# Products of constants ahead of the chains of layer 0's FFN and layer 2's routing

## The chip, the core and the metric

The kernel runs on one core of one Trainium2 chip. The metric is device time in microseconds (us) of that core for one execution; a kernel's time is the median of its runs.

## What is computed

Four layers work in turn on x of 4 x 512 x 128 numbers in float32. Each is FFN, attention, FFN, each with a residual. The change touches the two passes of layer 0's FFN and the two of layer 2's:

```python
# layer 0's FFN: three selections, one row per sequence of the batch (4 rows)
input_acts_seq = gelu(einsum('bsd,nd->bsn', x, input_patterns)).mean(axis=1)      # 4 x 1024
input_repr = the 128 largest of each row, zero elsewhere
process_acts = gelu(einsum('bn,pn->bp', input_repr, process_input_weights))       # 4 x 512
process_weights = softmax(the 64 largest of each row)
aggregated_value = einsum('bk,bkd->bd', process_weights, selected_process_values) # 4 x 64
output_acts_seq = gelu(einsum('bd,od->bo', aggregated_value, output_input_weights))  # 4 x 1024
out_per_seq = the 128 largest of each row, weighted sum of their output_patterns  # 4 x 128, to all 512 rows
# layer 2's FFN: each of the 2048 rows goes to the one expert of 8 with the largest probability
top1 = argmax(softmax(x @ router_w + router_b))
out = (a * sigmoid(g)) @ w2[top1] + b2[top1],  a, g = split(x @ w1[top1] + b1[top1])
```

## The kernel before, in words

The rows of x stand as 16 tiles of 128 rows by 128 features. All is float32; a float32 product of TensorE leaves two matmul records in the trace. PSUM is divided into banks of 128 x 512 by tag ("s": 4, "t": 2, "m": 2 in layer 0; "a": 2, "g": 2, "t": 2, "m": 2 in layer 2's FFN).

**Layer 0's FFN** (`l0_ffn`). For each sequence eight 512-column products (pa, through `mm_in_order`) are followed by a gelu on ScalarE that sums over the rows. Then the work is one chain for all four sequences:

- `largest` finds the 128 largest of each row of 1024. VectorE takes the eight largest of a list of 256 and strikes them out, 16 times (lines 386 to 390), merges the sorted lists (394 to 401), turns the limit by a small transpose on TensorE (pt_l, line 403), and settles ties by two 32-column products (place, 421 and 422).
- The selected values go through eight 512-column products on four groups of array columns (pp, line 440), two copies and one product that adds the four groups (pp again, 445).
- After a gelu on ScalarE, VectorE finds the 64 largest of 512 in eight rounds (451 to 456); softmax, a transpose (pt_w, 466), the products pg (472) and po (478), a gelu.
- `largest` once more, with the transpose pt_c (line 369) beside its first round; then po (484), a copy, and pb (489), which spreads the four results; VectorE adds them to x.

**Layer 2's FFN** (`l2_slots`). After the router's logits VectorE finds each row's expert as a one-hot (oh, line 1262) and a running count over tiles (cum). Three products give each row's position (pos, 1276 to 1278). From pos VectorE works out the expert of each of 23 slots of 128 rows (ei) and the place of each row in its slot (place, in_slot). Sixteen 23-column products then turn this around into the list of rows that come to each slot (pi, 1317; come, 1319). SyncE loads the weights of a slot's expert (line 1326, five buffers; needs ei), GpSimd fetches the slot's rows by indirect DMA (1330, four buffers; needs come), TensorE transposes them (pt_x) and multiplies.

**Order.** A scheduler orders the instructions of each engine, save those handed to `keep_in_program_order`, which keep the order in which the program states them. `mm_in_order` and `transpose_in_order` are so pinned, `mm` and `transpose` are not. `idle_product(tag, n)` is a product of constants (onesm and the first n columns of cst) into a bank that nobody reads; before the change only layer 1's attention calls it.

Of the kernel before, what the change touches and what calls it, by code (L numbers as in the profile page):

```python
# [28 lines left out]
P = 128  # L29
B, S, D, H, HD = 4, 512, 128, 16, 8  # L30
NT = B * S // P
# [72 lines left out]
def tile_macaron(ctx, tc, x_in, const_in, vec_in, w0_in, ws_in, ws3_in, w2f_in, w3_in, out):  # L104
# [17 lines left out]
    def bank(tag, name):  # L122
        n = 2 if tag == "d" else 1
        return psum["pool"].tile([P, n * 512], F32, tag=tag, name=name, bufs=psum["bufs"][tag])
# [31 lines left out]
    def const(name):  # L156
        return CONST(cst, name)
# [6 lines left out]
    def mm(dst, lhsT, rhs, start=True, stop=True):  # L164
        nc.tensor.matmul(dst, lhsT=lhsT, rhs=rhs, start=start, stop=stop)

    def transpose(dst, src):
        return nc.tensor.transpose(dst, src, ident[: src.shape[0], : src.shape[0]])  # L168

    def mm_in_order(dst, lhsT, rhs, start=True, stop=True):  # L170
        tc.keep_in_program_order(nc.tensor.matmul(dst, lhsT=lhsT, rhs=rhs, start=start, stop=stop))  # L171

    def transpose_in_order(dst, src):
        tc.keep_in_program_order(transpose(dst, src))

    def idle_product(tag, n):

        mm_in_order(bank(tag, "idle")[:, :n], onesm, cst[:, :n])

    def bcast(ap, n):  # L180

        return ap[:, :, None].to_broadcast([ap.shape[0], ap.shape[1], n])
# [161 lines left out]
    def l0_ffn(tag, chained):  # L344
        with pool(tag) as sb:
# [18 lines left out]
            def by_neuron(row, name):  # L364

                r = sb.tile([P, 8, B], F32, tag="by_n", name=name, bufs=2)
                pt = bank("t", "pt_c")
                for c in range(2):
                    transpose(pt[:, ts(c, P)], row[:, ts(c, P)])
                nc.vector.tensor_copy(  # L370
                    r.rearrange("p (q c) b -> p c q b", q=4),
                    pt[:, :256].rearrange("p (c q b) -> p c q b", c=2, q=4)[:, :, :, :B],
                )
                return r
# [7 lines left out]
            def largest(row, vals, r):  # L382

                w = sb.tile([P, 256], F32, tag="w256", name="w256")
                order = sb.tile([P, P], F32, tag="order", name="order")
                for i in range(P // 8):
                    m8, src = order[:, ts(i, 8)], w if i else row
                    nc.vector.max(m8, src)
                    if i < P // 8 - 1:
                        nc.vector.match_replace(w, m8, src, GONE)  # L390
                two = [sb.tile([64, P], F32, tag=f"two{i}", name="two") for i in range(2)]
                larger(two[0], order, 64, 64)
                for i in range(7):
                    halves = [t.rearrange("p (n i k) -> p n i k", i=2, k=64 >> i) for t in (two[i % 2], two[1 - i % 2])]
                    for to, op in enumerate((ALU.max, ALU.min)):
                        nc.vector.tensor_tensor(halves[1][:, :, to, :], halves[0][:, :, 0, :], halves[0][:, :, 1, :], op)
                turned = sb.tile([B, P], F32, tag="turned", name="turned")
                larger(turned, two[1], B, 32)
                limit = sb.tile([B, 1], F32, tag="limit", name="limit")
                nc.vector.tensor_reduce(limit, turned, AX.X, ALU.min)  # L400
                nc.vector.tensor_copy(turned, limit.to_broadcast([B, P]))
                pt = bank("t", "pt_l")
                transpose(pt[:, :B], turned)
                lim = sb.tile([P, B], F32, tag="lim", name="lim")
                nc.vector.tensor_copy(lim, pt[:, :B])
                above, equal = (sb.tile([P, 8, B], F32, tag=n, name=n) for n in ("above", "equal"))
                nc.vector.tensor_tensor(equal, vals, rows(lim, 8), ALU.is_equal)
                nc.vector.tensor_tensor(above, vals, rows(lim, 8), ALU.is_gt)
                many = sb.tile([P, B], F32, tag="many", name="many")
                nc.vector.tensor_reduce(many, above.rearrange("p c b -> p b c"), AX.X, ALU.add)  # L410

                sums = [sb.tile([P, 8, B], F32, tag=f"sums{i}", name="sums") for i in range(2)]
                nc.vector.tensor_copy(sums[0][:, 0, :], many)
                nc.vector.tensor_copy(sums[0][:, 1:, :], equal[:, :7, :])
                for i in range(3):
                    n, src, dst = 1 << i, sums[i % 2], sums[1 - i % 2]
                    nc.vector.tensor_copy(dst[:, :n, :], src[:, :n, :])
                    nc.vector.tensor_add(dst[:, n:, :], src[:, n:, :], src[:, : 8 - n, :])
                place = bank("m", "place")
                flat = lambda v: v.rearrange("p c b -> p (c b)")  # L420
                mm(place[:, : 8 * B], const("m1"), flat(equal), True, False)
                mm(place[:, : 8 * B], ones, flat(sums[1]), False, True)
                nc.vector.scalar_tensor_tensor(
                    equal, place[:, : 8 * B].rearrange("p (c b) -> p c b", b=B), float(P), equal, ALU.is_le, ALU.mult
                )
                nc.vector.tensor_add(above, above, equal)
                nc.vector.tensor_mul(r[:, :, :B], above, vals)

            pt = bank("t", "pt_a")
            for c in range(2):  # L430
                transpose(pt[:, ts(c, P)], acc[:, c, :, :].rearrange("p q b -> p (q b)"))
            nc.vector.tensor_scalar_mul(ra, pt[:, :256], 1.0 / S)
            vals = sb.tile([P, 8, B], F32, tag="by_n", name="vals", bufs=2)
            nc.vector.tensor_scalar_mul(vals.rearrange("p (q c) b -> p c q b", q=4), acc[:, :, :, :B], 1.0 / S)
# [2 lines left out]
            p4 = bank("m", "pp4")  # L437
            piw = W0(w0, "piw").rearrange("p (c n) -> p c n", n=512)
            for c in range(8):
                mm(p4[ts(c % 4, 32), :], kept[0][:, c, :], piw[:, c, :], c < 4, c >= 4)  # L440
            pq = sb.tile([P, 512], F32, name="pq4")
            nc.vector.tensor_copy(pq[:, 0:256], p4[:, 0:256])
            nc.vector.tensor_copy(pq[:, 256:512], p4[:, 256:512])
            pp = bank("m", "pp")
            mm(pp[:B, :], selb.rearrange("p (b n) -> p b n", n=P)[:, :, 0], pq)
            pa = sb.tile([B, 512], F32, name="pact")
            nc.scalar.activation(pa, pp[:B, :], AF.Gelu)

# [2 lines left out]
            for i in range(KP // 8):  # L451
                m8 = sb.tile([B, 8], F32, tag=f"m8{min(i, 1)}", name="m8", bufs=2)
                nc.vector.max(m8, w if i else pa)
                nc.vector.match_replace(w, m8, w if i else pa, GONE)
                if i == 0:
                    nc.vector.tensor_scalar_mul(nm, m8[:, 0:1], -1.0)
            ea = sb.tile([B, 512], F32, name="ea")
            nc.scalar.activation(ea, pa, AF.Exp, bias=nm)
            sm = sb.tile([B, 1], F32, name="sm")
# [3 lines left out]
            nc.vector.tensor_scalar_mul(pw, pw, sm)  # L463
            pt = bank("t", "pt_w")
            for c in range(4):
                transpose(pt[:, ts(c, B)], pw[:, ts(c, P)])
            pwT = sb.tile([P, 4, B], F32, name="pwT")
            nc.vector.tensor_copy(pwT, pt[:, : 4 * B].rearrange("p (n b) -> p n b", b=B))
            pg = bank("m", "pg")
            pv = W0(w0, "pv").rearrange("p (c n) -> p c n", n=64)  # L470
            for c in range(4):
                mm(pg[:64, :B], pv[:, c, :], pwT[:, c, :], c == 0, c == 3)
            nc.vector.tensor_copy(agg[:, :B], pg[:64, :B])

            oiw = W0(w0, "oiw")
            po = bank("m", "po0")
            for q in range(4):
                mm(po[ts(q, 32), :256], agg, oiw[:64, ts(q, 256)])
            nc.scalar.activation(oa, po[:, :256], AF.Gelu)
            largest(oa, by_neuron(oa, "out"), kept[1])  # L480
            po = bank("m", "po1")
            op = W0(w0, "op").rearrange("p (c n) -> p c n", n=D)
            for c in range(8):
                mm(po[ts(c % 4, 32), :D], kept[1][:, c, :], op[:, c, :], c < 4, c >= 4)
            o4 = sb.tile([P, D], F32, name="o4")
            nc.vector.tensor_copy(o4, po[:, :D])
            pb = bank("m", "pb")
            for b in range(B):
                mm(pb[:, ts(b, D)], selb[:, ts(b, P)], o4)

            def update(b):
                xb = x[:, ts(b, TB), :]
# [765 lines left out]
    def l2_slots(sb, ticks, gap):  # L1258
# [3 lines left out]
        oh = first_max(sb, g, "oh")  # L1262


        cum = [sb.tile([P, NT, 8], F32, name=f"cum{i}") for i in range(2)]
        src = oh
        for i in range(4):
# [5 lines left out]
        nc.vector.tensor_sub(before, src, oh)  # L1273
        pos = bank("m", "pos")
        flat = lambda v: v.rearrange("p t e -> p (t e)")
        mm(pos[:, 128:136], ones, src[:, NT - 1, :])
        mm(pos[:, 0:128], ones, flat(before), True, False)
        mm(pos[:, 0:128], const("m1"), flat(oh), False, True)

        ni = sb.tile([P, 8], I32, name="ni")  # L1280
        nf, base, end = (sb.tile([P, 8], F32, name=n) for n in ("nf", "base", "end"))
        nc.vector.tensor_scalar_add(ni, pos[:, 128:136], float(P - 1))
# [28 lines left out]
        in_slot = sb.tile([P, NT, SLOTS], F32, name="in_slot")  # L1311
        nc.vector.tensor_tensor(in_slot, rows(const("iota")[:, :SLOTS], NT), bcast(slot, SLOTS), ALU.is_equal)
        nc.vector.tensor_mul(in_slot, in_slot, bcast(const("row1"), SLOTS))
        pi = bank("m", "pi")
        for t in range(NT):
            nc.vector.tensor_scalar(in_place[:, t, :], const("iota"), place[:, t : t + 1], None, ALU.is_equal)
            mm(pi[:, :SLOTS], in_place[:, t, :], in_slot[:, t, :], t == 0, t == NT - 1)
        come = sb.tile([P, SLOTS], I32, name="come")
        nc.vector.tensor_scalar(come, pi[:, :SLOTS], -1.0, 0.0, ALU.add, ALU.max)

# [760 lines left out]
```

## Time and profile before

| | us |
|---|---|
| median of 3 runs | 2732.9 |
| lowest and highest run | 2726.75, 2735.28 |
| the profiled execution, its time | 2729.0 |
| its span, first to last instruction | 2726.9 |
| TensorE busy | 2191.1 |
| VectorE busy | 1808.4 |
| ScalarE busy | 1267.1 |
| mean granted TensorE clock | 0.88 |

The page of the profile cuts the span into 40 slices of some 68 us. Its digits are busy tenths; PEclk is the clock that TensorE was granted, in tenths of full speed. In the timeline each row has a start and a length in us, the engine (PE: TensorE's products, PEld: its weight loads, DVE: VectorE, ACT: ScalarE, POOL: GpSimd, SPq: SyncE's queue), the line, the operation with what it writes and reads, how many were merged, and in brackets the idle time before and who ended it. A matmul of the program is x2 there. The table of stretches gives for each stretch, after its length, the busy time of PE, PEld, DVE, ACT and POOL, then the granted clock, the mean share of the DMA engines and GB/s. The first pass of layer 0's FFN ends its products pa at about 50 us and pb at 126, the second at 308 and 384; layer 2's passes have their pos at 1218 and 1454.

### The profile page before, as it was taken

The page shows a single profiled execution, that of the slowest core. Times are in us where ns is not written, and L with a number is a line of the kernel's source. Part 1 is how long each engine was busy: PE and PEld are TensorE (multiplying, and loading weights), DVE is VectorE, ACT ScalarE, POOL GpSimd, SP SyncE. Part 2 cuts the span into 40 slices and gives each one's busy share as a digit, 9 for nine tenths or more (in the row PEclk, how much of TensorE's full clock was granted, in tenths as well). Part 3 has the DMA queues.
Part 4 walks back from the last instruction along what each step waited for, and adds up shares of the span by engine and source line. Part 5 has one row for each costly group of instructions (what it writes and reads, how often), then busy time and mean ns, then how long its engine had stood idle before and what let it go on. Part 6 is the DMA issues. An engine that isn't in the chain of part 4 may idle for free. (4 is left out here: it accounts for less than half of the span.)

```text
span 2726.9 us, 49905 instructions
## 1 busy us (share of the span) xinstructions
PE 2191.1 (80%) x18572; PEld 1226.1 (45%) x18572; DVE 1808.4 (66%) x5013; ACT 1267.1 (46%) x3067; POOL 905.4 (33%) x1678
## 2 busy tenths in 40 slices
PE   4277539988779999948666868898899999789888
PEld 2145214443334444438456745555433333455555
DVE  4746487777566777563664487777567775877774
ACT  3054314444333544314332356776525554667764
POOL 1012012233122222213321377766300000877761
PEclk8578769998789999868886889999879999899998
DMA  3053010000000000008104611000000000100000
GB/s 143 0 158 93 0 63 1 1 1 1 1 1 1 1 2 5 5 21 300 37 10 160 200 27 24 21 21 20 1 0 1 1 1 7 28 20 21 22 21 12
DMA packets 33930, 99.31 MB, mean 36 GB/s; under 512 B 6200, under 2 KB 12344, under 8 KB 33176
## 3 DMA queue, kind: packets, MB, share of 16 engines
q1 hardware_dynamic: 30760, 88.03, 10.0%
q0 software_dynamic: 2496, 5.12, 0.8%
q8 instruction: 146, 2.39, 0.4%
q10 hardware_dynamic: 432, 2.98, 0.3%
q14 instruction: 96, 0.79, 0.1%
HBM read 66.88 MB, written 14.55 MB: 30 GB/s over the span
## 5 line engine op out<-in xcount | busy, mean ns | idle before, releaser
L832 ACT ACTIVATE PT<-pk_at 128x512 f32<-128x512 f32 (+3 forms) x768 | 335.2, 488 | 405.4 <-PE pq_at L171 259.3
L171 PE MATMUL pk_at<-qx,km 32*128 32x512 f32 (+3 forms) x1536 | 398.8, 554 | 4.6 <-ACT PT L832 2.7
L804 DVE CUSTOM_DVE_ANT_0 s<-pq_at,cst 128x384 f32<-128x384 f32 (+3 forms) x512 | 249.9, 488 | 96.0 <-PE pq_at L171 42.5
L171 PE MATMUL pq_at<-km,qT 32*128 32x128 f32 (+3 forms) x1024 | 274.0, 500 | 16.0 <-DVE nm L804 12.0
L1607 ACT ACTIVATE s<-s,nm,rn 128x128 f32<-128x128 f32 x512 | 245.5, 482 | 0.9 <-DVE nm L1719 0.7
L835 POOL TENSOR_SCALAR_AFFINE_SELECT PT<-PT 128x256 f32<-128x256 f32 x256 | 104.5, 410 | 388.7 <-ACT PT L832 387.7
L171 PEld LDWEIGHTS pk_at<-qx,km 32*128 32x128 f32 x1536 | 146.7, 190 | 153.3 <-issue 92.9
L171 PE MATMUL po_at<-PT,vh 128*32 128x128 f32 (+3 forms) x2432 | 205.6, 394 | 8.5 <-POOL PT L835 8.4
L806 DVE TENSOR_REDUCE nm<-pq_at 128x1 f32<-128x512 f32 x256 | 165.6, 685 | 57.6 <-PE pq_at L171 57.2
L1668 POOL TENSOR_TENSOR t<-t,t 128x1024 f32<-128x1024 f32 x64 | 151.8, 2372 | 123.4 <-DVE t L1664 123.1
L171 PE MATMUL pq_at<-km,t 32*128 32x512 f32 x512 | 175.0, 670 | 1.6 <-DVE nm L806 1.2
L168 PE MATMUL pt_y<-ident,y 128*128 128x128 f32 x224 | 52.3, 362 | 132.2 <-DVE y L225 104.9
L171 PE MATMUL p_qk<-w,hT 128*128 128x512 f32 x256 | 141.9, 682 | 8.8 <-DVE t L1664 6.0
L254 ACT COPY yT<-pt_y 128x512 f32<-128x512 f32 x56 | 32.8, 585 | 239.1 <-PE pt_y L168 238.6
L168 PE MATMUL pt<-ident,s 128*128 128x128 f32 x640 | 93.0, 293 | 62.0 <-POOL s L1731 38.9
L1731 POOL TENSOR_TENSOR s<-s,sm 128x1024 f32<-128x1024 f32 x64 | 121.6, 1901 | 49.1 <-DVE sm L1730 41.0
L171 PEld LDWEIGHTS po_at<-PT,vh 128*32 128x32 f32 x2432 | 53.8, 109 | 173.3 <-issue 119.8
L171 PEld LDWEIGHTS pq_at<-km,qT 32*128 32x128 f32 x1024 | 110.2, 189 | 46.6 <-DVE nm L804 26.8
L1607 ACT ACTIVATE sq<-p_qk 128x1024 f32<-128x1024 f32 x64 | 65.6, 1026 | 118.4 <-PE p_qk L171 65.8
L168 PEld LDWEIGHTS pt<-ident,s 128*128 128x128 f32 x640 | 78.2, 150 | 93.7 <-POOL s L1731 48.1
L1661 DVE TENSOR_TENSOR t<-p_qk,w 128x1024 f32<-128x1024 f32 x64 | 78.2, 1223 | 55.7 <-ACT sq L1607 55.6
L1349 DVE SCALAR_TENSOR_TENSOR hT<-pa,w,sg 128x128 f32<-128x128 f32 x184 | 51.9, 345 | 85.4 <-ACT sg L1348 63.6
(435 smaller groups left out, 5167.6 us busy)
## 6 DMA issues: line engine op xcount, KB each, us to landing
w<-in_w2f_dram SPq DMA_DIRECT2D x46, 836.0 KB, 6.2
vb<-v SPq DMA_DIRECT2D x112, 128.0 KB, 2.2
skew<-qe SPq DMA_DIRECT2D x16, 512.0 KB, 3.0
rel<-skew SPq DMA_DIRECT2D x64, 128.0 KB, 3.5
w<-in_w_dram SPq DMA_DIRECT2D x1, 4147.0 KB, 12.5
w<-in_w_dram SPq DMA_DIRECT2D x1, 3200.0 KB
od<-o SPq DMA_DIRECT2D x46, 64.0 KB, 5.1
yd<-y SPq DMA_DIRECT2D x8, 256.0 KB, 2.3
```

What stands on the lines that cost most here:

```text
L168: return nc.tensor.transpose(dst, src, ident[: src.shape[0], : src.shape[0]])
L171: tc.keep_in_program_order(nc.tensor.matmul(dst, lhsT=lhsT, rhs=rhs, start=start, stop=stop))
L254: by_order(nc.scalar.copy(yT[:, b, :], pt))
L804: nc.vector.tensor_tensor_reduce(s[:, :nk], pq[:, :nk], causal[:, S - nk :], 1.0, -BIG, ALU.add, ALU.max, to)
L806: nc.vector.tensor_reduce(to, pq, AX.X, ALU.max)
L832: by_order(nc.scalar.activation(PT[:, i, q0:], pk[:, q0:], AF.Exp, scale=SC8))
L835: nc.gpsimd.affine_select(d, d, pattern=[[0, 2], [1, P]], base=0, channel_multiplier=-1, compare_op=ALU.is_ge, fill=0.0)
L1349: nc.vector.scalar_tensor_tensor(hT[s][:, c, :], pa[:, ts(c, P)], b1[:, c : c + 1], sg, ALU.add, ALU.mult)
L1607: tc.keep_in_program_order(nc.scalar.activation(*args, **kw))
L1661: nc.vector.tensor_mul(by_head(t1), by_head(p3), over(tab[:, 0]))
L1668: nc.gpsimd.tensor_add(t1, t1, t2)
L1731: nc.gpsimd.tensor_mul(s, s, bcast(sm, P))
```

## The change

A helper `warm(gate, n)` issues a small product that reads `gate`, and n 512-column `idle_product`s after it; all of them are pinned. As TensorE works in order, none starts before `gate` is written. It is called after the maxima of the last six of the 16 rounds of `largest`, with four more products behind the last; after the last four of the eight rounds of the selection of 64, with one more behind; and in the routing after oh (three), after pos (three, not gated) and after place (one). In layer 0 the banks are of tag "s", in layer 2 of tag "a". All products and transposes of these chains are now pinned too.

```diff
+    def warm(gate, n, tag="s"):
+
+        mm_in_order(bank(tag, "idle")[:, : gate.shape[1]], onesm[: gate.shape[0], :], gate)
+        for _ in range(n):
+            idle_product(tag, S)
+
...
                     nc.vector.max(m8, src)
                     if i < P // 8 - 1:
                         nc.vector.match_replace(w, m8, src, GONE)
+                    if i >= P // 8 - 6:
+                        warm(m8, 1)
+                for _ in range(4):
+                    idle_product("s", S)
...
-                transpose(pt[:, :B], turned)
+                transpose_in_order(pt[:, :B], turned)
...
-                mm(p4[ts(c % 4, 32), :], kept[0][:, c, :], piw[:, c, :], c < 4, c >= 4)
+                mm_in_order(p4[ts(c % 4, 32), :], kept[0][:, c, :], piw[:, c, :], c < 4, c >= 4)
...
                 if i == 0:
                     nc.vector.tensor_scalar_mul(nm, m8[:, 0:1], -1.0)
+                if i >= KP // 8 - 4:
+                    warm(m8, 1)
+            idle_product("s", S)
...
         oh = first_max(sb, g, "oh")
...
+        warm(oh[:, 0, :], 3, "a")
...
-        mm(pos[:, 128:136], ones, src[:, NT - 1, :])
-        mm(pos[:, 0:128], ones, flat(before), True, False)
-        mm(pos[:, 0:128], const("m1"), flat(oh), False, True)
-
+        mm_in_order(pos[:, 128:136], ones, src[:, NT - 1, :])
+        mm_in_order(pos[:, 0:128], ones, flat(before), True, False)
+        mm_in_order(pos[:, 0:128], const("m1"), flat(oh), False, True)
+
+        for _ in range(3):
+            idle_product("a", S)
...
         nc.vector.tensor_mul(in_slot, in_slot, bcast(const("row1"), SLOTS))
+        warm(place, 1, "a")
         pi = bank("m", "pi")
         for t in range(NT):
             nc.vector.tensor_scalar(in_place[:, t, :], const("iota"), place[:, t : t + 1], None, ALU.is_equal)
-            mm(pi[:, :SLOTS], in_place[:, t, :], in_slot[:, t, :], t == 0, t == NT - 1)
+            mm_in_order(pi[:, :SLOTS], in_place[:, t, :], in_slot[:, t, :], t == 0, t == NT - 1)
```

The other transposes and products of the two chains (pt_a, pt_c, pt_w, place, pg, po, pb and the second pp) are pinned in the same way.

More of the change, by code (lines that the diff above doesn't have):

```diff
@@ L368, in by_neuron @@
                 for c in range(2):
-                    transpose(pt[:, ts(c, P)], row[:, ts(c, P)])
+                    transpose_in_order(pt[:, ts(c, P)], row[:, ts(c, P)])
                 nc.vector.tensor_copy(
@@ L420, in largest @@
                 flat = lambda v: v.rearrange("p c b -> p (c b)")
-                mm(place[:, : 8 * B], const("m1"), flat(equal), True, False)
-                mm(place[:, : 8 * B], ones, flat(sums[1]), False, True)
+                mm_in_order(place[:, : 8 * B], const("m1"), flat(equal), True, False)
+                mm_in_order(place[:, : 8 * B], ones, flat(sums[1]), False, True)
                 nc.vector.scalar_tensor_tensor(
@@ L430, in l0_ffn @@
             for c in range(2):
-                transpose(pt[:, ts(c, P)], acc[:, c, :, :].rearrange("p q b -> p (q b)"))
+                transpose_in_order(pt[:, ts(c, P)], acc[:, c, :, :].rearrange("p q b -> p (q b)"))
             nc.vector.tensor_scalar_mul(ra, pt[:, :256], 1.0 / S)
@@ L444, in l0_ffn @@
             pp = bank("m", "pp")
-            mm(pp[:B, :], selb.rearrange("p (b n) -> p b n", n=P)[:, :, 0], pq)
+            mm_in_order(pp[:B, :], selb.rearrange("p (b n) -> p b n", n=P)[:, :, 0], pq)
             pa = sb.tile([B, 512], F32, name="pact")
@@ L465, in l0_ffn @@
             for c in range(4):
-                transpose(pt[:, ts(c, B)], pw[:, ts(c, P)])
+                transpose_in_order(pt[:, ts(c, B)], pw[:, ts(c, P)])
             pwT = sb.tile([P, 4, B], F32, name="pwT")
@@ L471, in l0_ffn @@
             for c in range(4):
-                mm(pg[:64, :B], pv[:, c, :], pwT[:, c, :], c == 0, c == 3)
+                mm_in_order(pg[:64, :B], pv[:, c, :], pwT[:, c, :], c == 0, c == 3)
             nc.vector.tensor_copy(agg[:, :B], pg[:64, :B])
@@ L477, in l0_ffn @@
             for q in range(4):
-                mm(po[ts(q, 32), :256], agg, oiw[:64, ts(q, 256)])
+                mm_in_order(po[ts(q, 32), :256], agg, oiw[:64, ts(q, 256)])
             nc.scalar.activation(oa, po[:, :256], AF.Gelu)
@@ L483, in l0_ffn @@
             for c in range(8):
-                mm(po[ts(c % 4, 32), :D], kept[1][:, c, :], op[:, c, :], c < 4, c >= 4)
+                mm_in_order(po[ts(c % 4, 32), :D], kept[1][:, c, :], op[:, c, :], c < 4, c >= 4)
             o4 = sb.tile([P, D], F32, name="o4")
@@ L488, in l0_ffn @@
             for b in range(B):
-                mm(pb[:, ts(b, D)], selb[:, ts(b, P)], o4)
+                mm_in_order(pb[:, ts(b, D)], selb[:, ts(b, P)], o4)
             def update(b):
```

## The prediction

> **What bounds the kernel now.** I read the page first, for the engines and the clock row; then the timeline of the four places that the diff touches; then the table of stretches, cut to the steps in which the clock moves.
>
> ```profile
> span 2726.9 us, 49905 instructions
> PE 2191.1 (80%) x18572; PEld 1226.1 (45%) x18572; DVE 1808.4 (66%) x5013; ACT 1267.1 (46%) x3067; POOL 905.4 (33%) x1678
> PEclk8578769998789999868886889999879999899998
> ```
>
> TensorE carries the span, but not here: in slice 2 it is busy 2 tenths at clock 5. The two layer 0 FFNs (50 to 126 us, and 308 to 384) and the two routings (1216 to 1237, and 1452 to 1473) are single chains, VectorE handing to TensorE and back, so each microsecond of either is a microsecond of the end. The timeline (start, length, engine, operation, in brackets the idle time before and who ended it):
>
> ```profile
> 61.10 0.43 DVE L388 MAX8 order<-w 128x8 f32<-128x256 f32 x1
> ...
> 70.62 0.21 DVE L401 COPY turned<-limit 4x128 f32<-4x128 f32 x1
> ...
> 70.89 0.26 PE L168 MATMUL pt_l<-ident,turned 4*128 4x4 f32 x1 [20.13 <-DVE turned L401]
> ...
> 74.55 3.64 PE L165 MATMUL pp<-w,kept 128*32 128x512 f32 x16 [0.85 <-PE place L165]
> ...
> 79.15 1.87 PE L165 MATMUL pp<-pq,cst 128*4 128x512 f32 x2 [0.96 <-DVE pq L443]
> ...
> 337.38 1.02 PE L165 MATMUL pp<-pq,cst 128*4 128x512 f32 x2 [0.96 <-DVE pq L443]
> ```
>
> pt_l comes after 20 us without a product. The last two rows are one product in the first FFN and in the second: 1.87 us at half clock, 1.02 us at full. That halving is all there is to win. When does the clock move? (Stretch, then busy time of PE, PEld, DVE, ACT, POOL, then PEclk.)
>
> ```profile
> 73.73:77.14 3.41, 2.59 (x16) 0.68 (x16) 0.57 (x3) 0.00 (x0) 0.00 (x0) 0.50 0.02 5
> 138.59:142.00 3.41, 3.41 (x5) 0.96 (x3) 2.33 (x7) 0.67 (x1) 0.00 (x0) 0.50 0.38 154
> 142.00:145.41 3.41, 0.83 (x5) 0.42 (x4) 1.86 (x7) 2.52 (x5) 0.00 (x0) 1.00 0.25 77
> 333.14:336.56 3.42, 3.28 (x16) 0.45 (x8) 0.08 (x1) 0.00 (x0) 0.00 (x0) 0.50 0.00 0
> 336.56:339.97 3.41, 1.02 (x2) 0.12 (x2) 1.55 (x5) 0.59 (x1) 0.00 (x0) 1.00 0.00 0
> ```
>
> All its changes lie on one grid of 3.41 us. At each grid point the stretch just ended decides: 3.28 us of products at half clock bring full clock, 2.59 don't; 1.02 or 0.83 us at full clock lose it. I weighted every product by its columns and its share of the 128x128 array and put all 793 stretches of the trace against the next one's clock: a limit at three quarters of what a stretch can hold at half clock is right in 786. So a stretch needs 2.56 us of full-array products at half clock to rise, 1.28 us at full clock to hold; weight loads and thin products count little.
>
> **The change, part by part.** All of it is on TensorE's queue. The instruction order of the two builds is the same on the other four engines; on TensorE only the new products come in, and pinning the chain's products moves none. VectorE gets two waits more per FFN (a maximum waits until the small product has read its buffer of two rounds ago); at the rounds below that product is over 1 us earlier, so nothing. What queues behind the new products is the chain's next product, as TensorE works in order.
>
> Prices: a 512-column product is two records; they start 1.71 us apart per product at half clock (138.59 to 140.30), 0.855 at full (ten records of pa in 4.45 us). A small one: 0.42 us at half (pos, 1217.78 to 1218.20), so 0.21; if half of its loads hide behind the product before, perhaps 0.12 (an estimate). I take 0.21, the row's.
>
> The ramp: the products start at any point of the grid step. With 2.56 us or more of it left (1 case in 4) the clock rises at its end, else one step later: after 2.6 to 6.0 us, mean 4.3.
>
> *First selection of 128.* From the first gated maximum (61.53) to pt_l's operand (70.83) are 9.3 us. Put in there: 6 x (0.21 + 0.855) + 4 x 0.855 = 9.8 us at full clock, and half of the ramp on top. TensorE is free 0.5 + ramp/2 too late: 1.8 to 3.5 us, mean 2.6 (2.1 with the small price of 0.12). The gain behind it, if the clock held: place 0.25, pp 3.64 to 1.9, the second pp 0.85: 2.85. But between the last large product and pp lie 3.4 us with only thin products. Stepping the queue through all grid positions, a point falls into that gap with under 1.28 us of large products behind it in about half of them, and pp starts at half clock again, to rise midway as in the second FFN of today. About 0.7 remains. Net +1.9.
>
> *Selection of 64.* Five large, four small: 5.1 us, from 88.32 to 95.05, which are 6.7: late by ramp/2 - 1.6, mean 0.6. Then pt_w (0.58), pg (1.01), po (1.08) and pt_c run close behind at full clock: half of each, 1.4 together. Net -0.8.
>
> *Second selection of 128.* Late by 2.6 again. Behind it place gives 0.25; po1 (1.08) and pb (2.08) would give 1.5. But the end of the ten products stands 8.5 to 6.8 us behind the rise (it is 9.8 - ramp/2), so the next grid points fall where one takes the clock before po1 starts, in nearly every position. Net +2.35. The attention behind starts 5.9 us after pb, at half clock before as after.
>
> One FFN: 1.9 - 0.8 + 2.35 = +3.4; two: +6.9.
>
> Here two rules of the Trainium skill speak, both in "TensorE: Matmul & The Clock Gate". Part 1, "The HAM clock gate": the warm-up is about 3.4 us of time, however many products. By it, the first selection would be late by 0.5 + 1.7 = 2.2, not 2.6: little change. The table "Why this matters for your kernels" asks for no gap over some 3 us; a 3.4 us gap would nearly pass, and the whole 2.85 and 1.5 come back: one FFN then +0.3. The trace decides against it: the step at 336.56 was not idle (1.02 us of products) and lost the clock all the same.
>
> *Routing, twice.* The first, and below it the DMA share (second number from the end) while the weights load.
>
> ```profile
> 1217.78 0.57 PE L165 MATMUL pos<-cum,ones 128*128 128x8 f32 x2 [5.43 <-DVE cum L1270]
> ...
> 1219.44 0.17 DVE L1282 TENSOR_SCALAR ni<-pos 128x8 int32<-128x8 f32 x1 [1.48 <-PE pos L165]
> ...
> 1223.75 7.02 PE L165 MATMUL pi<-in_slot,in_place 128*128 128x23 f32 x32 [4.35 <-DVE in_slot L1313]
> ```
>
> ```profile
> 1230.00:1232.00 2.00, 0.77 (x4) 0.64 (x4) 0.18 (x1) 0.00 (x0) 0.71 (x1) 0.50 1.00 418
> ```
>
> From oh (1216.11) to pos are 1.67 us; one small and three large need 2.8 + ramp/2. With pos itself halved (1.63 to 0.8) its end comes 1.6 to 3.5 us later, mean 2.5. The three after it (2.6) fit before place at +3.1, and the last pair (1.1) before in_slot at +4.3. pi, 32 records with a load each (0.97 us for eight at full clock in the slots), falls from 7.02 to 3.5 to 3.9, if no grid point takes the clock midway: it gives 1.0 to 3.5. The slot list so lands -1.3 to +1.6, mean 0. But the expert index hangs on pos too: the five first weight loads (836 KB each) start 2.5 us later, and they fill the DMA engines (share 1.00). The first token fetch today lands 5.6 us after its issue, with the loads' end (1236.88 and 1237.02), where unloaded ones take 2.6. With the loads ending later, the second fetch (1232.77 to 1237.23) takes the 5.6 too, and the first slot waits for it: 0.4 (second routing) to 1.1 more. +0.75 per routing, +1.5 for two.
>
> The sum: 6.9 + 1.5 = +8.4. On the profiled execution (2729.0 us: the span of 2726.9 and 2.1 around it) that is 2737.4; it lies 3.9 below the median of the three runs, and as the grid lies differently in each run, I apply the sum to the median: 2732.9 + 8.4, rounded 2741.
>
> **Rivals.**
> *Faster.* The mechanism is the hold over the 3.4 us gap. If thin products keep the clock, one FFN wins 2.85 + 1.4 + 1.75 = 6.0. Against it stand the lateness of 2.6 + 0.6 + 2.6 = 5.8; it decides from a ramp below 4.3 on. At the shortest, 2.6, the lateness is 1.8 + 0 + 1.8: -2.4 for each FFN, -1.3 for each routing: 2725.5. For: at 1159.17 a step with 1.7 us of products kept the clock. Against: 336.56 and 142.00. 0.15.
> *Does nothing.* Lateness and gain cancel, as by the rule above, and routing too: 2733. Speaks for it that they are of one size. 0.2.
> *Worse.* Long ramps everywhere, no hold, and the first slot 1.5 late: each FFN 3.5 + 1.4 + 3.5 - 1.65 = 6.75, each routing +2: 2750. 0.15.
> *The clock never rises* for these products: ten cost 17.1 + 2.5 instead of 9.3 us, +10 four times: past 2770. Every stretch full of 512-column products rose, so 0.02.
>
> **How the numbers follow.** The likeliest case, 2735 to 2746, has 0.48. Below 2724.7 (faster by 0.3%, about what a measurement of this kernel can tell from no change) lies half of the faster rival: 0.08. Above 2741.1 lie half of the likeliest and the two worse ones, and some of the likeliest with the small price doubled: 0.5. The rest is the same: 0.42. Range 2730 to 2750: it holds the likeliest, the no-change case and the mild end of the worse one.
>
> **What would show it.** In the profile after: pt_l waits for the engine's own product and starts 2 to 3.5 us after its operand; the stretch of the last four large products is at 1.00; pp in 3.64 or between, seldom 1.9; pt_w to po halved; pb still near 2.08; ni 2 to 3 us later behind oh; pi under 6 us; the first weight load later. It is wrong if pt_l isn't late (large products cheaper than pa's), or if pp and pb run at full clock in both FFNs.

## The result, and the profile after

The change makes the kernel slower. The median of 17 runs is 2745.15 us (2738.63 to 2754.45), that of 17 runs of the kernel before 2734.26 (2726.30 to 2743.29): the medians differ by +10.9 us. The ratio is 1.0043 with a 95% interval of 1.0030 to 1.0056, so a cost of 8 to 15 us. The prediction was +8.4 on the median of three runs then known, 2741. The page after, in the lines that answer to those shown of before:

```profile
span 2737.0 us, 50325 instructions
PE 2251.0 (82%) x18772; PEld 1248.3 (46%) x18772; DVE 1807.2 (66%) x5013; ACT 1266.1 (46%) x3067; POOL 904.3 (33%) x1678
PEclk9778869999889999879887879999889999899998
```

The products did raise the clock: the mean grant goes from 0.88 to 0.897, and the digits of the first slices from 857 to 977. The span grew by 10.1 us all the same. Two of its stages show why. First the first selection of 128, as a timeline:

```profile
63.67 2.05 PE L171 MATMUL idle<-cst,onesm 128*128 128x512 f32 x2
...
68.03 1.10 PE L171 MATMUL idle<-cst,onesm 128*128 128x512 f32 x2
...
69.11 4.54 PE L171 MATMUL idle<-cst,onesm 128*128 128x512 f32 x10
...
70.14 0.21 DVE L411 COPY turned<-limit 4x128 f32<-4x128 f32 x1
...
73.58 0.22 PE L168 MATMUL pt_l<-ident,turned 4*128 4x4 f32 x1
73.84 0.16 DVE L415 COPY lim<-pt_l 128x4 f32<-128x4 f32 x1 [3.48 <-PE pt_l L168]
```

VectorE has written pt_l's operand at 70.35. TensorE is then still in the row above: ten records, one gated product and the four behind it, until 73.65. So pt_l, which took 0.26 us after 20 us of idleness before, starts 3.2 us after its operand, and VectorE waits 3.48 us for it where it waited 0.36. Then the clock on its grid, in the columns of the prediction's table:

```profile
59.11:62.53 3.42, 1.44 (x3) 0.93 (x4) 3.21 (x11) 0.00 (x0) 0.00 (x0) 0.50 0.00 0
62.53:65.94 3.41, 3.41 (x9) 1.86 (x7) 3.17 (x11) 0.00 (x0) 0.00 (x0) 0.50 0.00 0
65.94:69.35 3.41, 3.41 (x14) 1.98 (x14) 3.06 (x18) 0.00 (x0) 0.00 (x0) 1.00 0.02 5
69.35:72.77 3.42, 3.42 (x9) 1.51 (x9) 0.90 (x4) 0.00 (x0) 0.00 (x0) 1.00 0.00 0
72.77:76.18 3.41, 1.84 (x8) 0.78 (x6) 1.67 (x13) 0.00 (x0) 0.00 (x0) 1.00 0.00 0
76.18:79.59 3.41, 2.68 (x16) 0.60 (x16) 0.54 (x3) 0.00 (x0) 0.00 (x0) 0.50 0.00 0
```

The ramp lasts from 61.09 to 65.94, 4.9 us. The clock is then full under the gated products, the four behind them and place, and gone at 76.18, just ahead of pp (76.91). What was bought with 3.1 us is mostly lost where it would have paid: pp takes 3.23 us instead of 3.64, and only the second pp behind it runs at full clock (1.02 us).

The milestones of both profiles give the account of each stage (us, from the start of one instruction to the start of the next; the two passes side by side). ra is VectorE's copy of the row means, with which the chain starts; turned and lim are the limit ahead of pt_l and behind it; kept are the selected values, pq the copy of the first pp, pact the gelu behind the second pp; pw and pwT are the softmax ahead of pt_w and behind it; oa is the gelu behind po, o the copy ahead of pb, x the addition at the end:

| stage | before | after | difference |
|---|---|---|---|
| turned to lim, first selection of 128 | 0.57, 0.57 | 3.70, 4.31 | +3.13, +3.74 |
| lim to pact (place, pp, second pp) | 9.85, 9.05 | 8.34, 8.65 | -1.51, -0.40 |
| pact to pw (selection of 64) | 13.53, 13.53 | 13.67, 13.67 | +0.14, +0.14 |
| pw to pwT | 1.15, 1.15 | 3.72, 3.88 | +2.57, +2.73 |
| pwT to the second turned (pg, po, pt_c) | 22.88, 22.88 | 21.81, 21.81 | -1.07, -1.07 |
| turned to lim, second selection | 0.63, 0.63 | 3.71, 3.78 | +3.08, +3.15 |
| lim to x (place, po, pb) | 6.99, 6.99 | 6.69, 6.68 | -0.30, -0.31 |
| layer 0's FFN, ra to x | 75.45, 74.64 | 81.47, 82.64 | +6.02, +8.00 |
| routing: oh to ni | 3.61, 3.62 | 6.23, 5.79 | +2.62, +2.17 |
| ni to come (pi) | 11.37, 11.37 | 8.10, 8.09 | -3.27, -3.28 |
| come to slot 0's first product | 7.01, 7.36 | 8.06, 9.08 | +1.05, +1.72 |

The sum is +14.0 for layer 0's FFN and +1.0 for routing. The span shows +10.1, as stages that the change doesn't touch came out 4.9 us shorter in sum in this execution (the attention of layer 0 took 180.1 instead of 182.7 us, all of layer 1 829.2 instead of 834.0; the stretch between layer 2's two routings took 3.2 us more). They scatter that much from profile to profile: layer 1 took 824.7 to 844.0 us in the twelve profiles of this study.

### The profile page after: what moved, and what is told of

Same layout as the page of the kernel before. It is cut to its first block, busy times and chain, and to the rows that moved or that the text cites. A ratio compares the mean times of both kernels' runs of the same rounds, so it can differ in the third digit from the quotient of the medians.

```text
span 2737.0 us, 50325 instructions
## 1 busy us (share of the span) xinstructions
PE 2251.0 (82%) x18772; PEld 1248.3 (46%) x18772; DVE 1807.2 (66%) x5013; ACT 1266.1 (46%) x3067; POOL 904.3 (33%) x1678
## 5 line engine op out<-in xcount | busy, mean ns | idle before, releaser
L171 PE MATMUL idle<-cst,onesm 128*128 128x512 f32 (+1 forms) x212 | 117.3, 662 | 3.2 <-DVE bkm L953 2.7
```

## The experiments

The theory: the new products hold TensorE's queue longer than VectorE leaves it free (lateness), and the clock that they raise is lost again in the gap between pt_l and pp, and between pt_l and po (lost hold). Rivals: W, the pinned order, the gates and their waits cost the time, whatever the products' length; R, the routing's late weight loads are the larger part; N, holding the clock would give nothing; D, the first fetch of a routing lands when the weight loads do, whatever comes before. Times are ratios to the kernel before on the same chip in the same session, whose median was 2718.98 to 2724.07 us in these three sessions.

### The pinned order alone, each half alone, and a filled gap

`pins` has none of the new products:

```diff
-                    if i >= P // 8 - 6:
-                        warm(m8, 1)
-                for _ in range(4):
-                    idle_product("s", S)
...
-                if i >= KP // 8 - 4:
-                    warm(m8, 1)
-            idle_product("s", S)
...
-        warm(oh[:, 0, :], 3, "a")
...
-        for _ in range(3):
-            idle_product("a", S)
...
-        warm(place, 1, "a")
```

> The changed kernel with all new products taken out; only the pinned order of the chains' own products and transposes is left. Theory (the new products hold TensorE's queue longer than VectorE leaves it free, and the clock they raise is lost again before it pays): no change, 2734 within 4 us, and in the profile each wait for TensorE as before: pt_l's result 0.57 us after its operand, pw to pwT 1.15, oh to ni about 3.6. Rival W (the pinned order itself and the waits that come with it cost the time): most of the 11 us of the change is here, 2742 or more.

Measured: 0.9993 (0.9981 to 1.0004); every stage of the table within 0.01 us of before up to x, and oh to ni 3.61. The pinning costs nothing, and this half of rival W falls.

`ffn` takes out the last three of those edits only (the routing's), `route` the first two.

> Only the products in layer 0's FFN; the routing as before but pinned. Theory: all of the loss is here. From ra to x the changed kernel's profile shows +6.0 and +8.0 us, so +10 to +14, 2744 to 2748; turned to lim again 3.1 us longer in all four selections of 128, pw to pwT 1 to 2.6 longer. Rival R (the routing's late weight loads are the larger part): under +5, below 2739.

> Only the products in the routing; layer 0's FFN as before but pinned. Theory: nearly nothing, because pos comes 2.5 to 4 us later and pi takes 3.4 less: -1 to +2 us, 2733 to 2736; oh to the first product of slot 0 within 1 us of the 22.0 and 22.3 of before. Rival R: +5 or more, 2739 and up, with the first slot starting over 2 us later behind oh.

Measured: `ffn` 1.0050 (1.0032 to 1.0068), which is +13.6 us; ra to x 81.44 and 82.62, the changed kernel's values to 0.03 us. `route` 1.0001 (0.9987 to 1.0016); oh to ni 6.33 and 6.14, ni to come 8.09 in both, oh to slot 0 22.25 and 22.89 against 21.99 and 22.34. The loss is all in layer 0's FFN, and rival R falls. The routing is a draw: what pi wins goes to the wait ahead of pos and to the fetch.

`hold` has the routing of `pins`, and this FFN:

```diff
                     if i >= P // 8 - 6:
                         warm(m8, 1)
-                for _ in range(4):
-                    idle_product("s", S)
...
                 transpose_in_order(pt[:, :B], turned)
+                idle_product("s", S)
...
                 mm_in_order(place[:, : 8 * B], const("m1"), flat(equal), True, False)
+                idle_product("s", S // 2)
                 mm_in_order(place[:, : 8 * B], ones, flat(sums[1]), False, True)
+                idle_product("s", S)
...
-                if i >= KP // 8 - 4:
+                if i >= KP // 8 - 3:
                     warm(m8, 1)
-            idle_product("s", S)
```

> Only layer 0's FFN, cut so that nothing is late: in the selections of 128 six gated rounds with one 512-column product each and none behind the last; a 512-, a 256- and a 512-column product put into the gap behind pt_l, behind the first place and behind the second; in the selection of 64 the last three rounds only and none behind. Theory: lateness gone (turned to lim under 1.5 us) and the gap filled, so that pp and po1 run at full clock: stepping the queue gives -3 us for each FFN (from -4.9 to -1.7), 2728 in all (2724 to 2731). Rival W (waits and gating cost, whatever the length): still over +5, 2739 or more. Rival N (the clock gives nothing here): 2734 with kept to pq still 4 us.

Measured: 0.9978 (0.9968 to 0.9989), 6 us faster than before. The timeline of TensorE in its first selection:

```profile
70.41 1.10 PE L171 MATMUL idle<-cst,onesm 128*128 128x512 f32 x2
71.45 0.22 PE L168 MATMUL pt_l<-ident,turned 4*128 4x4 f32 x1
71.60 1.12 PE L171 MATMUL idle<-cst,onesm 128*128 128x512 f32 x2
72.56 0.30 PE L171 MATMUL place<-equal,cst 128*128 128x32 f32 x2
72.70 0.68 PE L171 MATMUL idle<-cst,onesm 128*128 128x256 f32 x2
73.56 0.41 PE L171 MATMUL place<-sums,ones 128*128 128x32 f32 x2 [0.18 <-DVE sums L427]
73.80 1.10 PE L171 MATMUL idle<-cst,onesm 128*128 128x512 f32 x2
74.84 1.92 PE L171 MATMUL pp<-w,kept 128*32 128x512 f32 x16
```

pt_l follows the last gated product, 0.5 us later than before (turned to lim 1.05); the three products fill the gap with none of them late; and pp takes 1.92 us where it took 3.64. Behind the second selection po and pb run at full clock as well (kept to o 1.02 instead of 1.48, o to x 1.54 instead of 2.46). ra to x is 71.75 and 71.86: -3.7 and -2.8. Rival N falls, and W with it for the selections of 128: as many gates and waits there, and a gain.

### The two causes parted, the gates alone, the routing mended

`cut` is `hold` without the three products in the gap.

> As the kernel with the filled gap (hold), without the three products in the gap: six gated rounds with one 512-column product each in the selections of 128, three in the selection of 64, none behind. It parts the two causes. Theory (lateness and lost hold are two costs): turned to lim about 1.05 us as there, but pp and po1 find the clock gone again in part of the positions: kept to pq 3 to 4 instead of 2.3, o to x 2.46 instead of 1.54; each FFN 0 to +1 us against before, in all within 4 us of it. Rival N (the hold does not matter, only the lateness did): as fast as hold, -6 us.

Measured: 1.0006 (0.9991 to 1.0020). turned to lim 0.53 and 0.91: no lateness there, yet ra to x is 76.01 and 76.76, +0.6 and +2.1. kept to pq takes 3.52 and 3.88, o to x 2.46. What is left of the loss is the lateness of the selection of 64 (pw to pwT +2.3 and +1.9 against before); it outweighs what lim to pact gains (1.6 and 0.4). Without the lateness behind the selections of 128 the loss is mostly gone; without the hold no gain comes. Against `hold` it is 4.3 and 4.9 us, of which the stages behind the gap explain 2.2 in the first pass (kept to pq 1.22, kept to o 0.38, o to x 0.92, lim to kept 0.23, less 0.52 at pt_l); the rest lies in the selection of 64 (pw to pwT 3.41 instead of 1.75, pwT to oa 2.72 instead of 2.33), where its three pairs, the same in both kernels, met the grid elsewhere: in `hold` the stretch from 88.52 to 91.94 counts 0.76 of what half clock can hold, by the weighting of the prediction, and brings full clock; in `cut` none of the three stretches under the pairs does (0.41, 0.60, 0.49). So both causes are there, and that part is the grid's position.

`thin` keeps the gates of the changed FFN and drops the large products:

```diff
                     if i >= P // 8 - 6:
-                        warm(m8, 1)
-                for _ in range(4):
-                    idle_product("s", S)
+                        warm(m8, 0)
...
                 if i >= KP // 8 - 4:
-                    warm(m8, 1)
-            idle_product("s", S)
+                    warm(m8, 0)
```

> The changed FFN with the gated small products alone: no 512-column product at all; routing as before, pinned. It measures the gate, its waits on both engines and the small products. Theory: they cost nothing by themselves (VectorE waits 0.14 us per FFN in the selection of 64), the clock stays at one half: within 3 us of before, turned to lim 0.57, pw to pwT 1.15. Rival W: +3 us or more.

Measured: 0.9988 (0.9968 to 1.0008); turned to lim 0.57, pw to pwT 1.15, pact to pw 13.67, as expected. What is left of rival W falls: the gates alone cost nothing that these runs can show. VectorE's extra wait is 0.14 us per FFN, and the changed kernel has just that.

`early` has no product in layer 0, and moves three in the routing:

```diff
         g = routed.pop("g")
+        warm(g[:, 0, :], 3, "a")
         softmax8(sb, g)
         oh = first_max(sb, g, "oh")
...
-        warm(oh[:, 0, :], 3, "a")
```

> Only the routing, with the three products in front of pos moved ahead of the softmax, gated by the logits (1212.6 in the profile before) instead of by oh (1216.1); the three behind pos and the one behind place stay. Layer 0 as before, pinned. Theory: the three, 5.5 us at half clock, are done when pos needs TensorE (1217.8), so oh to ni is no longer 6.2 but 2.8 to 4, ni to come stays near 8.1, the weight loads start no later, and the first slot starts 2 to 3.5 us earlier behind oh than before: -4 to -7 us for two routings, about 0.998 of before. Rival D (the first fetch lands with the weight loads, whatever come does): come 3 us earlier, the first slot not: within 2 us of before.

`both` is the FFN of `hold` with this routing:

> The filled gap in layer 0's FFN (hold) and the moved products in the routing (early) together, meant to beat the kernel before and the changed one. Theory: the gains add, -6 and -4 to -7: 0.996 of before. By rival D: -6 alone, 0.998.

Measured: `early` 0.9988 (0.9973 to 1.0003). oh to ni fell to 2.94 in both passes, ni to come to 8.09 and 8.46, and slot 0 starts 19.03 and 19.69 us behind oh, 3.0 and 2.7 earlier than before. That is the expected gain in the stage; 5.6 us in sum are not clear of the scatter in the time. Rival D falls by the profile: the first fetch landed 17.35 us behind oh instead of 21.06, the fourth of the five weight loads only at 19.54. `both` 0.9962 (0.9948 to 0.9975), some 10 us below the kernel before, where the changed kernel is 11 above it; both gains stand in its profile (ra to x 71.65 and 71.86, oh to slot 0 18.91 and 20.04). It beats the kernel before and the changed one. TensorE behind its second selection:

```profile
120.16 1.10 PE L171 MATMUL idle<-cst,onesm 128*128 128x512 f32 x2
121.20 0.65 PE L171 MATMUL po<-w,kept 128*32 128x128 f32 x16
122.26 1.16 PE L171 MATMUL pb<-o,cst 128*128 128x128 f32 x8 [0.41 <-DVE o L499]
```

against the changed kernel in the same place, where there is nothing between place and po and both run at half clock:

```profile
126.95 0.41 PE L171 MATMUL place<-sums,ones 128*128 128x32 f32 x2 [1.01 <-DVE sums L428]
128.17 1.08 PE L171 MATMUL po<-w,kept 128*32 128x128 f32 x16 [0.81 <-DVE kept L437]
129.66 2.08 PE L171 MATMUL pb<-o,cst 128*128 128x128 f32 x8 [0.41 <-DVE o L499]
```

### The limit of three quarters, and the selection of 64

`half` is `ffn` with 256 columns for 512 in the products of the selections of 128:

```diff
                     if i >= P // 8 - 6:
-                        warm(m8, 1)
+                        mm_in_order(bank("s", "idle")[:, :8], onesm, m8)
+                        idle_product("s", S // 2)
                 for _ in range(4):
-                    idle_product("s", S)
+                    idle_product("s", S // 2)
```

> The changed FFN with 256 instead of 512 columns in the products of the selections of 128 (number, gates and those of the selection of 64 unchanged), routing as before. It tests the limit of three quarters. Theory: at half clock a pair now takes 0.42 + 0.86 = 1.28 us, of which 0.86 counts, 67 of 100: the stretches under the six rounds stay at 0.50 though TensorE is busy throughout, and only the four behind can raise the clock. turned to lim 1.5 to 2.4 us in the selections of 128 (3.7 in the changed kernel). Rival (any busy stretch raises the clock, as the busy time reads): a stretch under the rounds is followed by 1.00, and turned to lim falls below 1.0.

Three stretches of its first selection, from the second gated product to place, and two of its second:

```profile
63.31:66.72 3.41, 3.41 (x13) 2.96 (x12) 3.13 (x12) 0.00 (x0) 0.00 (x0) 0.50 0.02 5
66.72:70.14 3.42, 3.42 (x10) 2.79 (x11) 3.08 (x17) 0.00 (x0) 0.00 (x0) 0.50 0.00 0
70.14:73.55 3.41, 1.92 (x11) 1.31 (x9) 1.71 (x13) 0.00 (x0) 0.00 (x0) 1.00 0.00 0
...
114.51:117.92 3.41, 3.41 (x12) 2.87 (x12) 3.17 (x12) 0.00 (x0) 0.00 (x0) 0.50 0.00 0
117.92:121.34 3.42, 3.42 (x20) 3.10 (x19) 3.11 (x16) 0.00 (x0) 0.00 (x0) 1.00 0.02 5
```

In the first TensorE is busy all the time, with pairs of which two thirds count (0.69 by the weighting), and the clock stays at half; in the second the products behind the last round come in (0.84), and it rises. In the changed kernel a stretch as busy, with 512 columns (62.53 to 65.94, 0.86), raised it. But the forecast failed in one selection of four: from 114.51 to 117.92 pairs that count 0.71 were followed by full clock, and turned to lim was 0.53 there, which is the rival's sign. Eight stretches of the four selections were busy throughout at half clock. The three that count 0.84 and more all raised the clock; of the five that count 0.66 to 0.71 four did not. So busy time alone does not decide, and the limit is known no closer than 0.7 to three quarters. turned to lim was 1.54 and 1.72 in the first selections, as forecast, 0.53 and 2.60 in the second, outside the forecast on either side.

This kernel ran once. Its time, 2756.05 us, is 37 above before, of which the two FFNs explain 12 (ra to x 80.10 and 82.02), and most of that is the selection of 64: with its products unchanged, pw to pwT took 6.09 us in both passes instead of 3.72 and 3.88, as the clock rose later under them. The rest stands outside the changed stages (layer 1 took 844.0 us), and is not explained.

`no64` is `both` with no product in the selection of 64:

> The fast version (both) without any product in the selection of 64. Theory: these three pairs pay nothing: VectorE's 0.25 us (pact to pw 13.53 again) and pw to pwT 1.15 instead of 1.6 are won, pwT to oa 2.71 instead of 2.33 is lost: -0.3 us for each FFN, not to be told from both by time (0.996 of before). If they did pay, it would be slower by over 2 us.

Measured: 0.9968 (0.9955 to 0.9982), the same as `both`; ra to x 70.96 and 71.63, -0.7 and -0.2 against it (0.5 of the first lies at turned to lim of the first selection, ahead of those pairs). They don't pay: they win 0.39 at pg and po and cost more ahead of pt_w.

This profile also answers whether `hold` gained only because its chain met the grid elsewhere. ra of the first pass starts 3.26 us behind a grid point in `hold`, but 1.04 in `no64`, close to the 1.26 of `cut`. kept to pq is 2.30 in `no64` as in `hold`, against 3.52 in `cut`. In all six passes with the filled gap (`hold`, `both`, `no64`) it is 2.30, so the filling holds the clock, and not the position.

## Why the prediction was right, point by point

- **What bounds these stages**: right. With the two FFNs' chains 6.0 and 8.0 us longer, and nothing else touched, `ffn` is 13.6 us slower.
- **The grid, and its limit of three quarters**: right within what can be told. The limit forecasts 780 of the 796 stretches of the profile after; limits on plain busy time, chosen for the best fit, forecast 753. Any limit from 0.70 to 0.76 does about as well (777 to 786), and `half` has one stretch at 0.71 that rose.
- **Lateness of the selections of 128**, 1.8 to 3.5 us, mean 2.6: right in kind, but too small; 3.1, 3.7, 3.1 and 3.2 were measured. The ramp came out longer than its mean (4.9 us in the first; half of it and 0.5 are 2.9), and longer than the 3.4 us of the rule cited there. The prediction reckoned it as if the large products came without a break, 2.56 us of them. A gated pair takes 2.13 us and counts 1.71 of it, so 2.56 us need 3.2, and the mean ramp is 4.9 (an estimate from these figures).
- **The lost hold**: right. Of 2.85 behind the first selection 1.5 and 0.4 came (0.7 was forecast, the second pp at full clock among it), and of 1.5 at po and pb 0.1. The Trainium skill asks only that TensorE have no idle gap of over some 3 us between matmul bursts ("TensorE: Matmul & The Clock Gate", section "Why this matters for your kernels"). By that the clock would have lasted, as the longest idle time between the last large product and pp is 1.01 us, and one FFN would have come to -0.2 by the prediction's own terms (5.8 late, 6.0 gained; the +0.3 written there does not follow from them). The measured clock, gone at 76.18 after a stretch with 1.84 us of busy time, decides against it here.
- **The selection of 64**, late by 0.6 and net -0.8: wrong; this is the step that failed. It was late by 2.6 and 2.7, net +1.6 and +1.8. A pair was priced as in the other selections, 2.13 us at half clock, and there it takes that:

```profile
61.54 2.06 PE L171 MATMUL idle<-cst,onesm 128*128 128x512 f32 x2
62.53 0.34 PEld L171 LDWEIGHTS idle<-order,onesm 128*128 128x128 f32 x1 [0.52 <-DVE w L396]
63.38 0.34 PEld L171 LDWEIGHTS idle<-order,onesm 128*128 128x128 f32 x1 [0.52 <-issue]
```

  The first load of the small product comes under the large one, a microsecond before its end. In the selection of 64, where the gated maxima have four rows and not 128, a pair takes 2.53:

```profile
89.50 0.50 PEld L171 LDWEIGHTS idle<-m,onesm 4*128 4x128 f32 x2 [8.29 <-DVE m L463]
90.02 0.50 PEld L171 LDWEIGHTS idle<-cst,onesm 128*128 128x128 f32 x2
92.03 0.50 PEld L171 LDWEIGHTS idle<-m,onesm 4*128 4x128 f32 x2 [1.50 <-DVE w_proc L464]
92.55 0.50 PEld L171 LDWEIGHTS idle<-cst,onesm 128*128 128x128 f32 x2
94.55 0.50 PEld L171 LDWEIGHTS idle<-m,onesm 4*128 4x128 f32 x2 [1.50 <-DVE m L463]
```

  The loads of a small product stand idle for 1.50 us, through most of the large product before it, and come only when it is over: gate to gate 2.53 us. The gates named had long been open. With 1.71 us of each 2.53 counting (68 of 100), a stretch full of such pairs reaches the limit only where it happens to hold parts of three large products. The first below counts 0.64 and keeps half clock, the second 0.77 and brings full clock, so the ramp lasts 7.2 us, to 96.66. It is a matter of position too: the same products were late by 4.9 us in `half`.

```profile
89.83:93.25 3.42, 3.42 (x7) 1.67 (x7) 3.21 (x7) 0.00 (x0) 0.00 (x0) 0.50 0.01 2
93.25:96.66 3.41, 3.41 (x6) 1.00 (x4) 2.76 (x8) 0.00 (x0) 0.00 (x0) 0.50 0.00 0
96.66:100.07 3.41, 3.14 (x16) 1.56 (x15) 0.17 (x1) 0.00 (x0) 0.00 (x0) 1.00 0.00 0
```

- **No cost on VectorE**: nearly; 0.14 us per FFN.
- **Routing**, +0.75 each: right in sum, and nearly in its parts. pos +2.6 and +2.2 (2.5 forecast), the slot list -0.65 and -1.1 (mean 0 forecast), the first slot behind it +1.05 and +1.72 (1.1 and 0.4 forecast), in all +0.4 and +0.6. In the second routing two misses, -1.1 and +1.3, cancel; that is luck.
- **The sum**, +8.4: the FFNs' +14.0 instead of +6.9 stand in the profile, and the missing 7 are mostly the selection of 64 (5.0 of them); the rest is lateness of the selections of 128 above its mean (2.7 in sum), less 0.6 of gains above theirs. So the number came out better than its parts. The stages of the profile cost 15.0 us, nearly twice the +8.4, and stages outside, which scatter, took back 4.9 in that execution. The runs leave open whether the true cost is nearer 10.9 or 15: both lie within 8 to 15, and `ffn` alone gave 13.6. That 8.4 lies so near 10.9 is in part luck; the sign and the two causes are not.

## What to carry to other kernels

Products that only keep TensorE's clock up are work in an in-order queue: add up their length at half clock for the ramp, at full after it, and compare with the time until the chain's next operand. Any excess is paid at once. Their gain comes only if the clock lasts to the costly product, so put some of them into the short waits that the chain has anyway, right in front of that product, instead of all into the long wait ahead of them. Here that turned +13.6 us into -6.

## What the runs showed that was not expected

A product on four rows beside products on 128 rows cost 0.4 us more per pair at half clock than one on 128 rows (2.53 instead of 2.14 from one gate to the next); its weight load came only after the large product. That the four rows are the reason is not shown: no run changed the rows alone.

The clock's grid does not lie at random against the program: ra of the first FFN starts 0.96 to 1.46 us behind a grid point in eight of the twelve profiles of before, the changed kernel and the experiments, and the second pass's within a band of 0.7 us in all. So the same stages meet it alike from run to run, and a mean over all positions, as in the prediction, is only a stand-in.
